# A graph network with LSTM windows on one core: block turns by VectorE and DMA, and seven-product LSTM steps summed in PSUM

## The chip, the cores and the metric

The kernel runs on one core of one Trainium2 chip, everything in 32-bit floats. The metric is the device time of one launch in microseconds; for the kernel before it is the median of three runs. A second number is the span of one profiled execution, from its first to its last instruction; the durations of single instructions all come from that execution.

## What is computed

The input `x` is 128 batches of 64 nodes with 256 features, with one 64 x 64 matrix `adj` for all. Four layers follow each other, each with a residual and a normalisation over the features:

```python
x = _layernorm(x + _L0_gnn_ref(x, adj, adj, W1, W2, W3))        # three products with adj*adj
x = _layernorm(x + _L1_gnn_ref(x, adj, W1, b1, W2, b2))         # eigenvectors U of a Laplacian
x = _layernorm(x + _L2_gnn_ref(x, adj, Wg0, ..., bih, bhh))     # two graph steps, then LSTMs
x = _layernorm(x + _L3_gnn_ref(x, adj, W, b_lin, b))            # attention over the 64 nodes
```

The LSTM part of the third layer is the largest. For p = 1, 2, 3, 4 in turn the 64 nodes of a batch are cut into windows of p rows; a one-layer LSTM with weights of its own runs over the p rows of each window, and its last hidden state replaces the window's last row:

```python
for p in range(1, MAX_SKIP + 1):
    wins = h[:, :nw * p, :].reshape(Bv * nw, p, Hd)
    last = _lstm_last(Wih[p - 1], Whh[p - 1], bih[p - 1], bhh[p - 1], wins)
    h = h.at[:, jnp.arange(nw) * p + (p - 1), :].set(last.reshape(Bv, nw, Hd))
```

One step is `g = x_t @ Wih.T + h @ Whh.T + bias`, split into the gates i, f, g, o, and then `c = sig(f)*c + sig(i)*tanh(g)`, `h = sig(o)*tanh(c)`. The first step of a window has no h and no old c, so it needs only i, g and o.

## The kernel before, in words

All 8192 rows (batch times node) are cut into 16 groups of 512 rows, four tiles of 128 rows each. The kernel has two stages. The first, to about 861 us, is layer 0 for all groups, with the eigenvectors worked out on VectorE beside it. The second takes the groups through layers 1, 2 and 3; the change is there alone.

In the second stage nothing is issued at once. `unit` records the work of two groups (the last four groups are units of one) as operations with a cost and the tiles they read and write; `Plan.run` then picks, engine by engine, the operation that can start earliest by its own account of times, with at most three units under way, and issues it. So the order of instructions on every engine is fixed when the program is built. Tiles live in a fixed number of slots per kind: 8 PSUM banks (`ps`), work tiles of 1024 columns (`w`, `WIDE` of them) and of 512 (`v`), `gates`, `c`, `hs`, and two attention tiles (`att`). `MOST` says how many of a kind are kept for the oldest unit. DMAs of this stage are issued from SP, in the planned order. All planned instructions carry line 156, so the profile's groups are told apart by tiles and shapes.

For a group, `layer1` multiplies with the eigenvectors (tiles `u2`, `ut2`). `to_lstm` makes `hT`, the features on the partitions and (node, batch) along a row. `lstm(hT, p, first, nw)` runs the windows of p rows step by step: for each gate and each half h of the 256 hidden features, two matmuls with `wih` and, from the second step on, two with `whh`, into a bank of its own; ScalarE reads the bank with the bias and applies tanh (the sigmoids are written through tanh), and VectorE does the rest. p = 1 is done in two calls of 256 columns, p = 2 in 256 columns, p = 3 in 168, and p = 4 in 128 columns per group.

For the second step of p = 2, and for steps two to four of p = 4 in units of two groups (`four`), `halves` takes the place of the direct matmuls. It cuts weights (two halves of inputs, two of outputs) and columns (two halves w) into a 2 x 2 block product and forms it from seven products instead of eight: sums of weight blocks are made once (`add_weights`), sums of the moving operands each step on VectorE, and the products go two to a bank, where ScalarE (`u1`) or VectorE picks them up and adds them into the `gates` tile.

Afterwards `from_lstm` brings `hT` back to rows: two copies on VectorE and two on ScalarE reorder it, eight TensorE transposes (a transpose is a TensorE instruction with `ident`, into a bank) turn it, and VectorE adds it to the rows. `layer3` needs three more turns: 8 transposes for `xT`, 8 for `hn` (the rows of h, with the bias `d_b` added) and 4 for the attention weights `e`, each with a copy or an add out of a bank. `norm` forms the statistics on VectorE and the root on GpSimd.

Of the kernel before, what the change touches and what calls it, by code (L numbers as in the profile page):

```python
# [99 lines left out]
class Op:  # L100
    __slots__ = ("engine", "calls", "cost", "lag", "before", "left", "after", "tiles", "start", "group", "rank", "ready", "unit")


class Plan:
# [7 lines left out]
    MOST = {"w": 4, "v": 2, "ps": 4, "gates": 2, "hs": 2}  # L112
# [11 lines left out]
    def note(self, engine, calls, cost, ready=0.0):  # L124
# [5 lines left out]
        for name, args, kw in () if callable(calls) else calls:  # L130
            for i, x in enumerate(list(args) + list(kw.values())):
                if not isinstance(x, Part):
                    continue
                t, write = x.tile, i == 0
                mask = np.zeros(int(np.prod(t.shape[1:])), bool)

                mask[... if t.tag == "ps" and not write else x.at.reshape(-1)] = True
                for other, w, rows, m in t.past:
                    if (w or write) and other is not op and other.start is None and rows[0] < x.rows[1] and x.rows[0] < rows[1] and (m & mask).any():
                        op.before.add(other)  # L140
                t.past.append((op, write, x.rows, mask))
                if t not in op.tiles:
                    op.tiles.append(t)
                    t.left += 1
        op.left = len(op.before)
# [12 lines left out]
    def run(self, units, ways):  # L158
# [4 lines left out]
        def rank(op):  # L163
            if op.engine == "PE" and not todo and len(left) <= LASTS:
                return -left[op.group]
            return op.group or 99

        def candidates(guard):
            oldest = min([u for u in going if u] or [0])
            best = None  # L170
            for e, ops in able.items():
                first = []
                for op in ops:
                    t = max(self.free[e], op.ready)
                    for tile in op.tiles:
                        if tile.real is None and tile.slot is None:
                            s = self.slots[tile.tag]
                            t = max(t, min(s))

                            if (guard and op.unit != oldest and  # L180
                                    sum(x < 1e9 for x in s) <= self.MOST.get(tile.tag, 1) - held.get((oldest, tile.tag), 0)):
                                t = 1e9
# [9 lines left out]
        while todo or going:  # L192
            while todo and len(going) < ways + (0 in going):
# [3 lines left out]
                going[self.unit] = len(self.ops)  # L197
                for op in self.ops:
# [544 lines left out]
GATES = 5  # L743
# [3 lines left out]
LASTS = 3  # L747
SINGLE = 4

# [58 lines left out]
def kernel(  # L808
# [92 lines left out]
    sqT2 = keep.tile([P, P], F32, name="sqT2")  # L901
    rs_row = keep.tile([P, P], F32, name="rs_row")
# [9 lines left out]
    dbl = load(keep, "dbl", d_bl, "p (k o) -> p k o", [P, 2, 1], o=1)  # L912
    cb1 = keep.tile([P, 2], F32, name="cb1")
# [209 lines left out]
    V.tensor_copy(rs_row, pr[:, :P])  # L1123
    V.tensor_reduce(rs_col, adst, AX.X, ALU.add)
    V.tensor_scalar(wide["c_b0"], wide["c_b0"], rs_col, None, op0=ALU.mult)
    V.tensor_add(cbi, cbi, cbh)
    for q in (slice(0, 4), slice(6, 8)):
# [23 lines left out]

    def place(tag, slot, shape):
        if tag == "att":
            return att[slot][:, :shape[1], :]
        if tag == "ps":
            return tl(psb, shape, f"ps{slot}")
        if tag in ("w", "v", "gates", "c", "hs"):
# [4 lines left out]
                {"ps": 8, "w": WIDE, "v": 4, "gates": GATES, "c": CELLS, "hs": OUTS, "att": ATT, "mx": 4, "sm": 4, "st": 4, "mv": 4,  # L1162
# [8 lines left out]
    def quarters(w):  # L1171
        w = w.rearrange("p k (a b h m) -> p k a b h m", a=2, b=2, h=2)
        return [w[:, k, :, b] for b in range(2) for k in range(2)]

    ways = {}

    def add_weights(p, ready):
        ways[p] = []
        for k, w in enumerate((wih[p - 1], whh[p - 1])):

            i = int(p == 2 and k == 1)
            s = wb.tile([P, 4 - i, 2, 2, P], F32, name=f"sums{p}{k}")
            s, w = plan.tile("sums", [P, 4 - i, 2, 2, P], s), plan.tile("sums", [P, 2, 1024], w)
            a11, a12, a21, a22 = quarters(w)
            S1, S2, S4, S3 = [s[:, j] for j in range(4 - i)] + [a21] * i
            V.tensor_add(S1, a21, a22, ready=ready)
            V.tensor_sub(S2, S1, a11, ready=ready)
            V.tensor_sub(S4, a12, S2, ready=ready)
            V.tensor_sub(S3, a11, a21, ready=ready)
            ways[p].append([a11, a12, a22, S1, S2, S3, S4])  # L1190

    def products(calls):
# [3 lines left out]
        plan.note("PE", [("matmul", (o, l, r), {"start": a, "stop": z}) for o, l, r, a, z in calls], cost)  # L1196
# [35 lines left out]
    def norm(x, scalar):  # L1232
# [4 lines left out]
        G.tensor_scalar(rs, mv[:, :, 1], EPS, None, op0=ALU.add)  # L1237
# [12 lines left out]
    def layer1(xs):  # L1250
# [14 lines left out]
        for t in range(0, 4, 2):  # L1265
# [4 lines left out]
            norm(xs[:, t:t + 2, :], False)  # L1270

    def to_lstm(xs):
        a = mixed(xs, adT2)
# [16 lines left out]
        for p, first, nw in ((1, 0, 32), (1, 32, 32), (2, 0, 32), (3, 0, 21)):  # L1290
            lstm(hT, p, first, nw)
        return hT

    def from_lstm(xs, hT, g):
        hb = as3(work(), 2)
        for bs in (slice(0, 4), slice(4, 8)):
            for k, copy, cost in ((0, V.tensor_copy, 0.33), (1, S.copy, 0.56)):
                copy(as3(hb[:, k, :], 8)[:, bs, :], hT[:, k, :, bs].rearrange("p n b -> p b n"), cost=cost)
        for t in range(0, 4, 2):
            p = ps4((P, 2, D))  # L1300
            turns([(p[:, j, k * P:(k + 1) * P], hb[:, k, (t + j) * P:(t + j + 1) * P]) for j in range(2)
                   for k in range(2)])
            V.scalar_tensor_tensor(xs[:, t:t + 2, :], p, 0.5, xs[:, t:t + 2, :], op0=ALU.mult, op1=ALU.add)
            norm(xs[:, t:t + 2, :], g in ENDING)

    def layer3(xs, g, first, nt):

        tiles = range(first, first + nt)

# [6 lines left out]
        xT = part(work(), 2)  # L1316
        ps = [ps4() for _ in range(2)]
        for t in tiles:
            turns([(ps[k][:, cols(t)], xs[:, t, k * P:(k + 1) * P]) for k in range(2)])
        if g in ENDING:  # L1320
            S.copy(xT[:, 0, :], ps[0][:, :nt * P])
        else:
            V.tensor_copy(xT[:, 0, :], ps[0][:, :nt * P])
        S.copy(xT[:, 1, :], ps[1][:, :nt * P])
        hT = part(work(), 2)
        for c in range(2):
            p = ps4()[:, :nt * P]
            run(p, [(dw[:, k, c * P:(c + 1) * P], xT[:, k, :]) for k in range(2)])
            S.activation(hT[:, c, :], p, AF.Identity, bias=dbl[:, c, :])
        p = ps4((P, nt, N))  # L1330
# [15 lines left out]
        V.tensor_sub(s, s, mx.unsqueeze(2).to_broadcast([P, nt, N]))  # L1346
        e = plan.tile("att", [P, nt, P])
        for h in range(2):
            hs = slice(h * N, (h + 1) * N)
            S.activation(e[hs, :, hs], s[hs, :, :], AF.Exp, cost=0.215 + 0.00042 * nt * N)  # L1350
        hn = part(work(), nt)
        for t in range(0, nt, 2):
            p = ps4((P, 2, D))
            turns([(p[:, j, c * P:(c + 1) * P], hT[:, c, (t + j) * P:(t + j + 1) * P]) for j in range(2)
                   for c in range(2)])

            V.tensor_add(hn[:, t:t + 2, :], p, wide["d_b"].unsqueeze(1).to_broadcast([P, 2, D]))
        sm = plan.tile("sm", [P, 4])[:, :nt]
        p = ps4()[:, :nt * P]
        turns([(p[:, t * P:(t + 1) * P], e[:, t, :]) for t in range(nt)])  # L1360
        eT = work2()[:, :nt * P]
        S.copy(eT, p)
        V.tensor_reduce(sm, e, AX.X, ALU.add)
        V.reciprocal(sm, sm)
        for t in range(0, nt, 2):
            p = ps4((P, 2, D))
            for j in range(2):
                run(p[:, j, :], [(eT[:, (t + j) * P:(t + j + 1) * P], hn[:, t + j, :])])
# [4 lines left out]
            norm(x2, g in ENDING)  # L1373
# [4 lines left out]
    def lstm(hT, p, first, nw, c=None, new=None):  # L1378
# [5 lines left out]
        only, hs = c is not None, None  # L1384
        for t in range(1 if only else p):
# [4 lines left out]
            if p == 2 and t:  # L1390
                x = [[xt[k][:, 16 * w:16 * w + 16] for w in range(2)] for k in range(2)]
                halves(2, x, hs.rearrange("p k (w n) -> p k w n", w=2), c.rearrange("p h (w n) -> p h w n", w=2), None,
                       lambda h, w: hT[:, h, 32 * w + 1:32 * w + 32:2, :])
                return
# [4 lines left out]
            if p > 1 and not t and not only:  # L1399
                c = plan.tile("c", [P, 512])[:, :2 * n].rearrange("p (h n) -> p h n", h=2)  # L1400
            if not only:
                new = None if last else plan.tile("hs", [P, 512])[:, :2 * n].rearrange("p (h n) -> p h n", h=2)
            for h in range(2):
                for q in names:
# [12 lines left out]
                    if q == "g":  # L1417
                        to = gate[h]["g"] if t or p == 1 else c[:, h, :]
# [7 lines left out]
                        S.activation(gate[h]["i"], c[:, h, :] if p > 1 else to, AF.Tanh, scale=0.5)  # L1426
# [12 lines left out]
    def halves(p, x, hs, c, new, rows):  # L1439
# [3 lines left out]
        bias = cbi[:, p - 1, :]  # L1443

        G = [plan.tile("gates", [P, 1024]).rearrange("p (w m q n) -> p w m q n", w=2, m=2, q=2) for _ in range(2)]
        both = work().rearrange("p (s i n) -> p s i n", s=2, i=4)

        def eights(v):
            return v.rearrange("p (w b) -> p w b", b=8)

        y = [[eights(hs[:, k, w]) for w in range(2)] for k in range(2)]
# [146 lines left out]
```

## Time and profile before

| | us |
|---|---|
| three runs: lowest, median, highest | 2457.69, 2458.52, 2458.81 |
| span of the profiled execution | 2455.8 |
| busy ScalarE, 860 to 1000 us | 72.19 of 140.00 |
| busy VectorE, 860 to 1000 us | 84.40 of 140.00 |
| busy TensorE, 2200 to 2400 us | 200.00 of 200.00 |
| one copy of 128x512 out of a bank: VectorE, ScalarE | 0.683, 0.583 |
| one add of 128x256 from a bank into `gates`, VectorE | 0.417 |
| one activation of 128x256 out of a bank, ScalarE | 0.473 |
| out rows, 128 KB, from issue to landing | 1.8 |
| `rest<-XA` and `X<-rest`, 512 KB, from issue to landing | 2.6, 3.3 |

Rows of the profile name an engine (PE is TensorE, PEld its weight loads, DVE VectorE, ACT ScalarE, POOL GpSimd, SP the queue that issues DMAs), the busy time in us and, after an x, the number of instructions. A matmul of 32-bit floats appears as two instructions, a transpose as one. TensorE's instructions overlap, so the duration of one is longer than the distance to the next.

### The profile page before, as it was taken

The page shows a single profiled execution, that of the slowest core. Times are in us where ns is not written, and L with a number is a line of the kernel's source. Part 1 is how long each engine was busy: PE and PEld are TensorE (multiplying, and loading weights), DVE is VectorE, ACT ScalarE, POOL GpSimd, SP SyncE. Part 2 cuts the span into 40 slices and gives each one's busy share as a digit, 9 for nine tenths or more (in the row PEclk, how much of TensorE's full clock was granted, in tenths as well). Part 3 has the DMA queues.
Part 4 walks back from the last instruction along what each step waited for, and adds up shares of the span by engine and source line. Part 5 has one row for each costly group of instructions (what it writes and reads, how often), then busy time and mean ns, then how long its engine had stood idle before and what let it go on. Part 6 is the DMA issues. An engine that isn't in the chain of part 4 may idle for free.

```text
span 2455.8 us, 40814 instructions
## 1 busy us (share of the span) xinstructions
PE 2431.6 (99%) x15500; PEld 2158.3 (88%) x15500; DVE 1618.6 (66%) x5676; ACT 1073.0 (44%) x2610; POOL 137.5 (6%) x315
## 2 busy tenths in 40 slices
PE   9999999999999999999999999999999999999997
PEld 7888888878887899989989998998998998988996
DVE  6888877778888265584684486477558458374336
ACT  2333433333333354445444445444444444545555
POOL 0000000000000010010010000001001001010002
PEclk9999999999999999999999999999999999999999
DMA  7000000000000020010000001001001000000000
GB/s 227 9 1 18 9 10 10 9 10 9 9 1 1 35 87 1 1 36 1 1 18 18 1 1 35 1 1 36 1 1 35 1 1 18 1 10 1 1 1 27
DMA packets 27972, 42.69 MB, mean 17 GB/s; under 512 B 2944, under 2 KB 22144, under 8 KB 27776
## 3 DMA queue, kind: packets, MB, share of 16 engines
q1 hardware_dynamic: 27424, 39.81, 4.7%
q8 instruction: 122, 2.00, 0.3%
q14 instruction: 74, 0.61, 0.1%
q10 hardware_dynamic: 352, 0.28, 0.0%
HBM read 26.45 MB, written 13.63 MB: 16 GB/s over the span
## 4 chain that ended last, share of the span: by engine, by line
PE 94%; DVE 4%; DMA 1%; ACT 0%; issue 0%; POOL 0%; SPq 0%; ACTq 0%; POOLq 0%; DVEq 0%
PE ps L156 62%; PE ps L940 31%; DVE D L52 1%; DVE X L156 1%; PE pc L296 1%; DMA XA<-in_x_dram 1%; DVE st L156 0%; DVE tw L52 0%; POOL rs L156 0%; DVE w L156 0%; DVE h L52 0%; ACT gates L156 0%; DVE gates L156 0%; DVE u L52 0%; DVE v L156 0%
## 5 line engine op out<-in xcount | busy, mean ns | idle before, releaser
L156 PE MATMUL ps<-w,wih 128*128 128x128 f32 (+2 forms) x4144 | 752.7, 315 | 0.9 <-DVE gates L156 0.9
L156 PEld LDWEIGHTS ps<-w,wih 128*128 128x128 f32 x4144 | 646.5, 191 | 37.0 <-issue 6.7
L156 ACT ACTIVATE gates<-ps,cbi 128x168 f32<-128x168 f32 (+2 forms) x832 | 342.2, 417 | 361.2 <-PE ps L156 353.0
L156 PE MATMUL ps<-hs,whh 128*128 128x168 f32 (+1 forms) x1952 | 345.1, 291 | 0.0
L156 PEld LDWEIGHTS ps<-hs,whh 128*128 128x128 f32 x1952 | 288.9, 191 | 1.2 <-issue 1.0
L156 PE MATMUL ps<-w,sums 128*128 128x128 f32 x1776 | 237.7, 275 | 0.0
L940 PE MATMUL ps<-aw,h 128*128 128x256 f32 x1024 | 227.2, 379 | 0.0
L156 DVE SCALAR_TENSOR_TENSOR gates<-gates 128x256 f32<-128x256 f32 (+2 forms) x220 | 83.9, 382 | 215.7 <-ACT gates L156 215.1
L156 PEld LDWEIGHTS ps<-w,sums 128*128 128x128 f32 x1776 | 218.1, 192 | 1.5 <-issue 1.2
L940 PEld LDWEIGHTS ps<-aw,h 128*128 128x128 f32 x1024 | 192.9, 190 | 25.9 <-ACT h L949 0.5
L156 ACT ACTIVATE gates<-gates,cbi 128x256 f32<-128x256 f32 x272 | 116.2, 497 | 194.6 <-DVE gates L156 194.6
L949 ACT ACTIVATE h<-h 128x512 f32<-128x512 f32 x128 | 80.4, 629 | 196.3 <-DVE h L52 196.1
L156 DVE TENSOR_TENSOR gates<-gates,ps 128x256 f32<-128x256 f32 x340 | 128.4, 417 | 19.4 <-PE ps L156 14.4
L940 PE MATMUL ps<-ss,tw 128*128 128x256 f32 x512 | 117.9, 380 | 0.0
L940 PE MATMUL ps<-ss,aw 128*128 128x256 f32 x512 | 117.3, 379 | 0.0
L940 PE MATMUL ps<-m,aw 128*128 128x256 f32 x512 | 117.1, 380 | 0.0
L156 DVE SCALAR_TENSOR_TENSOR c<-gates,c 128x256 f32<-128x256 f32 (+2 forms) x156 | 57.1, 366 | 87.2 <-ACT gates L156 87.0
L940 PE MATMUL ps<-aw,m 128*128 128x512 f32 x256 | 114.6, 593 | 0.0
L156 DVE TENSOR_TENSOR gates<-v,ps 128x256 f32<-128x256 f32 x136 | 55.6, 417 | 80.7 <-ACT v L156 49.9
L940 PEld LDWEIGHTS ps<-ss,aw 128*128 128x128 f32 x512 | 96.6, 190 | 12.8
L940 PEld LDWEIGHTS ps<-ss,tw 128*128 128x128 f32 x512 | 96.3, 190 | 12.9 <-issue 0.2
L940 PEld LDWEIGHTS ps<-m,aw 128*128 128x128 f32 x512 | 95.6, 190 | 12.6 <-issue 0.5
(314 smaller groups left out, 3734.7 us busy)
## 6 DMA issues: line engine op xcount, KB each, us to landing
out_dram<-X SPq DMA_DIRECT2D x64, 128.0 KB, 1.8
rest<-XA SPq DMA_DIRECT2D x10, 512.0 KB, 2.6
X<-rest SPq DMA_DIRECT2D x10, 512.0 KB, 3.3
XA<-in_x_dram SPq DMA_DIRECT2D x18, 256.0 KB, 6.0
wih<-in_c_ih_dram SPq DMA_DIRECT2D x4, 1024.0 KB, 7.4
aw<-in_a_w_dram SPq DMA_DIRECT2D x3, 1024.0 KB, 10.8
X<-in_x_dram SPq DMA_DIRECT2D x12, 256.0 KB, 5.9
whh<-in_c_hh_dram SPq DMA_DIRECT2D x3, 1024.0 KB, 9.4
```

The lines of the kernel that those rows point to most:

```text
L52: return getattr(self.engine, name)(out, *args, **kw)
L156: getattr(e, name)(*[real(x) for x in args], **{k: real(v) for k, v in kw.items()})
L296: PE.matmul(out, lhsT, rhs, start=True, stop=True)
L940: PE.matmul(out, lhsT, rhs, start=start, stop=stop)
L949: S.activation(dst, src, AF.Relu)
```

## The change

Two things change, both in the second stage.

First, in the 14 groups that are not in `ENDING`, TensorE's transposes are replaced. VectorE's transpose turns each 32 x 32 block of a tile by itself; the blocks are then put in order by DMA: `across` writes the tile to a buffer in device memory (`far`, eight of them) and reads it back in four pieces into another work tile. `from_lstm` does so once, `layer3` twice, and for the attention weights eight small DMAs place the turned blocks straight into the `att` tile. The softmax is now formed on the unturned tile.

Second, the seven-product form is used for all steps but p = 3 (and p = 4 in the four units of one group): for p = 1, for both steps of p = 2 and all four of p = 4. `fast` replaces `halves`. It sums inside the banks: product 1 goes into `chain`, ScalarE copies it out for a first block, product 6 is added on top in the same bank, it is copied out again, then 7, an add, then 4. A second bank takes product 2, a third 5 and then, on top, 3. Products go in gate by gate, all gates of a pass side by side in one bank. The four planned numbers for slots and the rank by which the planner picks (`due`, a time before which an operation should start, counted in `PERIOD` per group) change with it. Smaller edits: a factor of one half moves into `adH2` and the normalisation, `dbb` adds two biases, and a list of plain ordering edges is given to the leftover normalisations of the first stage.

```diff
-    MOST = {"w": 4, "v": 2, "ps": 4, "gates": 2, "hs": 2}
+    MOST = {"w": 3, "v": 2, "ps": 2, "gates": 3, "hs": 2}
...
-            return op.group or 99
+            return op.due
...
+                for op in reversed(self.ops):
+                    op.tail = op.cost + max([x.tail + (self.OWN if x.engine == op.engine else self.LAG)[op.engine]
+                                             for x in op.after] or [0.0])
+                    op.due = op.group * PERIOD - op.tail
...
-GATES = 5
+NARROW = 3
+GATES = 6
+PERIOD = 25.0
+FARS = 8
...
+    def across(src):
+        far = plan.tile("far", [P, 1024])
+        Q.dma_start(far, src, cost=0.6)
+        dst = work()
+        for j in range(4):
+            Q.dma_start(dst[32 * j:32 * j + 32].rearrange("r (i f) -> r i f", i=4),
+                        seen(far[:, 256 * j:256 * j + 256], "(i r) f -> r i f", i=4), cost=0.6)
+        return dst
...
+        z = work()
+        for k in range(2):
+            V.transpose(z.rearrange("p (j t k f) -> p t j k f", j=4, t=4, k=2)[:, :, :, k],
+                        hT[:, k].rearrange("p n b -> p b n"))
+        y = across(z).rearrange("p (i m f) -> p m i f", i=4, m=8)
...
-        for p, first, nw in ((1, 0, 32), (1, 32, 32), (2, 0, 32), (3, 0, 21)):
-            lstm(hT, p, first, nw)
+        singles(hT)
+        pairs(hT)
+        lstm(hT, 3, 0, 21)
...
+            S.activation(s, s, AF.Exp)
+            V.tensor_reduce(sm, s, AX.X, ALU.add)
+            z = sc.rearrange("p a c -> p (a c)")[:, 256:]
+            V.transpose(z.rearrange("p (b t r) -> p t b r", b=2, t=4), s)
+            for h in range(2):
+                for b in range(2):
+                    for a in range(2):
+                        Q.dma_start(e[64 * h + 32 * b:64 * h + 32 * b + 32, :, 64 * h + 32 * a:64 * h + 32 * a + 32],
+                                    z[64 * h + 32 * a:64 * h + 32 * a + 32, 128 * b:128 * b + 128]
+                                    .rearrange("p (t r) -> p t r", t=4), cost=0.6)
...
-            p1, p2 = two(0, 1)
-            S.copy(u1, p1)
-            V.tensor_add(a, u1, p2)
-            p6, p7 = two(5, 6)
-            V.tensor_add(c12, u1, p6)
-            V.tensor_add(b, c12, p7)
-            p5, p3 = two(4, 2)
-            V.tensor_add(d, b, p5)
-            V.tensor_add(c12, c12, p5)
-            V.tensor_add(c12, c12, p3)
-            p4, _ = two(3)
-            V.tensor_add(b, b, p4)
+            chain, bank2, bank5 = ps4(shape), ps4(shape), ps4(shape)
+            c11, c12, c22 = block[0][:, :, 0], block[0][:, :, 1], block[1][:, :, 1]
+            product(chain, 1, qs, True, (block[0], bank2))
+            S.copy(c11, chain)
+            product(bank2, 2, qs, True)
+            V.tensor_add(c11, c11, bank2)
+            product(chain, 6, qs, False)
+            S.copy(c12, chain)
+            product(bank5, 5, qs, True)
+            S.copy(c22, bank5)
+            product(chain, 7, qs, False)
+            V.tensor_add(c22, c22, chain)
+            product(bank5, 3, qs, False)
+            V.tensor_add(c12, c12, bank5)
+            product(chain, 4, qs, False)
...
+        fast(1, 256, [[hT[:, k, 32 * w:32 * w + 32, :] for w in range(2)] for k in range(2)], write=write)
...
+        fast(2, 128, x[0], c=c, new=hs)
+        fast(2, 128, x[1], hs=hs, c=c, write=write)
...
-        for w in range(2):
-            lstm(hTs[w], 4, 0, 16, c[:, :, w, :], hs[:, :, w, :])
-        for t in range(1, 4):
+        for t in range(4):
             x = [[hTs[w][:, k, t:t + 61:4, :] for w in range(2)] for k in range(2)]
             new = state("hs") if t < 3 else None
-            halves(4, x, hs, c, new, lambda h, w: hTs[w][:, h, 3:64:4, :])
+            fast(4, 128, x, hs, c, new, write)
             hs = new
```

## The prediction, made before the run

> **What bounds the kernel now.** I read the page's span and busy shares first, then the busy time by stretches, then the waits of TensorE alone, then the groups kept apart by shape, last the timeline of TensorE for the true distance between matmuls.
>
> ```profile
> span 2455.8 us, 40814 instructions
> PE 2431.6 (99%) x15500; PEld 2158.3 (88%) x15500; DVE 1618.6 (66%) x5676; ACT 1073.0 (44%) x2610; POOL 137.5 (6%) x315
> PE 94%; DVE 4%; DMA 1%; ACT 0%; issue 0%; POOL 0%; SPq 0%; ACTq 0%; POOLq 0%; DVEq 0%
> ...
> 1000.00:2200.00 1200.00, 1197.85 (x8703) 1104.53 (x8702) 761.44 (x2240) 555.41 (x1320) 77.88 (x156) 1.00 0.03 11
> 2400.00:2456.00 56.00, 40.12 (x329) 33.08 (x327) 39.98 (x137) 28.96 (x71) 15.00 (x40) 0.91 0.09 29
> ...
> PE ps L156 <- DVE w L156: 1.0, 3, 0.4
> PE ps L156 <- DVE gates L156: 0.9, 1, 0.9
> ```
>
> TensorE is busy 2431.6 of 2455.8 us at full clock, and 94% of the chain that ended last is TensorE. The stretch from 1000 to 2200 us has 1197.85 of 1200 us busy, with VectorE at 63% and ScalarE at 46%. The last two lines are all of TensorE's waits between 860 and 2400 us: 1.9 us. So there the time is the sum of the matmuls. The one loose place is the last 56 us, where TensorE idles 15.9 us: the last groups alone, one dependency after another.
>
> A busy row alone could hide pipelining, so I take the cost of a matmul from the distance between starts:
>
> ```profile
> 958.96 9.66 PE L156 MATMUL ps<-w,wih 128*128 128x256 f32 x44
> 968.46 1.46 PE L156 MATMUL ps<-bw,v 128*128 128x256 f32 x6
> ...
> 1017.02 2.84 PE L156 MATMUL ps<-w,wih 128*128 128x128 f32 x24
> 1019.70 1.50 PE L156 MATMUL ps<-adT,w 128*128 128x128 f32 x12
> ...
> 2404.76 1.91 PE L156 MATMUL ps<-ident,w 128*128 128x128 f32 x16
> 2406.51 0.61 PE L156 MATMUL ps<-w,wih 128*128 128x128 f32 x4
> ```
>
> 256 columns: (968.46 - 958.96)/44 = 0.216 us; 128 columns: 2.68/24 = 0.1117 us; a transpose: 1.75/16 = 0.109 us. A matmul of the program is two of these instructions (1152 records of the 256-column form for 576 in the built program), so 0.4315 us and 0.2234 us; a transpose is one. Priced so, everything TensorE has after the first `u2` matmul at 860.96 us comes to 1585 us; it took until 2442.57 us, 1581.6 us. The prices hold to 0.2%.
>
> [...]
>
> **The change, part by part, on TensorE.** Counts are from the two built programs.
> - p = 1 (`singles`): 24 matmuls of 256 columns per group become 7 products x 3 gates = 21: 16 groups x 3 x 0.4315 = -20.7 us.
> - p = 2, first step: 12 of 256 become 21 of 128, 16 x (12 x 0.4315 - 21 x 0.2234) = -7.8 us.
> - p = 4, first step of six units: 24 of 128 become 21, -18 x 0.2234 = -4.0 us.
> - The later steps of p = 2 and p = 4 had seven products already: 0. p = 3 and the p = 4 steps of the four single groups stay as they are: 0.
> - Transposes: per group 8 in `from_lstm`, 8 + 8 + 4 in `layer3`; 28 x 14 groups x 0.109 = -42.7 us.
>
> Sum: **-75.2 us** of TensorE work.
>
> **On the other engines**, which must only stay below TensorE. VectorE: 428 gate sums of 256 columns out of a bank go (0.417 us: -178); 150 of 512 (0.68) and 66 of 384 (0.55, between its neighbours) come (+139). The block turns are 56 of 512 and 70 of 256 columns; taken like a 512-column pass (0.68) and a 256-column one (0.41), +67 us; bounds: [...] twice my price, +134. The copies and adds after TensorE's transposes go (-42); operand sums for the new seven-product steps come (+52); the pointwise gate operations become fewer and wider (-18). Net some +20 us on 1619. ScalarE: 264 copies out of banks come (0.365 to 0.585 us, +136) for 68 that go (-25), gate activations in other sizes (+18), fewer copies after transposes (-20); net some +110 us on 1073, which takes it from 46% to about 56% in the steady stretch, VectorE from 63% to about 67%. Neither bounds.
>
> **Waits that come.** First, the bank re-entries: 88 passes (32 for p = 1, 32 for p = 2, 24 for p = 4) x 4 = 352 places where a product goes into a bank that ScalarE or VectorE has just read. Behind the waiting matmul stands all of TensorE's order. The reader starts about 0.21 us after the last matmul (in before, matmuls ending at 1001.29 by distance, the activation at 1001.50) and takes 0.585 (copy of 512) or 0.68 us (add), so 0.8 to 0.9 us must be filled. In the built order I summed the matmuls between each bank's last write before a read and its next write: the median is 1.2 us above the need, and only 3 of 352 fall short, by 1.2 us in all. That assumes a reader that is free at once. Low end 0; high end a mean 0.3 us each, 106 us; I take 3 us, since readers at 56% and 67% will sometimes be a little late and 17 places have under 0.1 us to spare.
>
> Second, the turns: 42 of them, each a write of 512 KB (2.6 us by the row of `rest<-XA`) and four reads of 128 KB (the row `X<-rest`, 512 KB, took 3.3), and 14 times eight small copies into the attention tile, at 0.37 to 0.47 us each to issue on SP by the four weight loads at 860 us: about 3.4 us plus 1.9 to land. All are issued in order on SP, where a turn that waits for its write holds up the next group's turns, the output rows and the reload of X, and behind those stand the group's own products. A group's way lengthens by some 3 x 6 us minus what the transposes and copies took. While it waits, TensorE has two other units of two groups each; before, it idled 2 us in 1540 with the same number. The turns move 42 x 1.05 = 44 MB, 28 GB/s over the 1530 us in question, beside 227 GB/s in the first slice: bandwidth is no issue. Low end 0, high end one half turn per group uncovered, 14 x 2.5 = 35 us; I take 3.
>
> Third, the end: groups 14 and 15 keep TensorE's transposes, so the same chain closes the kernel, but in the built order all 56 of their transposes now stand after the last LSTM matmul, with 27 us of TensorE work there. I take 4 us more idle there (between 0 and 8). At the start, the sums of the weights of p = 1 are 8 short VectorE operations, under 5 us, while TensorE has layer 1 of several groups: 0.
>
> **Sum.** 2455.8 - 75.2 + 3 + 3 + 4 = 2390.6 us for the span. The median lies 2.7 us above the profiled span, so **2393 us**.
>
> **Rivals.**
> 1. Nothing is given back: 2458.5 - 75.2 = 2383 us. For it: the fill computed above. Against: the planned order assumes transfers and readers on time. 0.13.
> 2. The turns take the place of the transposes: one half turn per group uncovered, 2383 + 35 + 10 = 2428 us. For it: SP's single order, seven large work tiles that are now held while DMAs land. Against: the present 2 us of waits. 0.16.
> 3. Slower: the bank reads. TensorE stops at each of the 352 re-entries until ScalarE or VectorE has read; from a mean stop of 75/352 = 0.21 us on the gain is gone, and at 0.3 us the time is 2383 + 106 = 2489 us. For it: ScalarE's longer queue, and an order that cannot move aside. Against: the fill, and single stops must be large to make that mean. 0.10.
>
> My forecast has 0.61, its own range 2384 to 2412.
>
> **How the numbers follow.** The range runs from 2378 (rival 1 with a little less at the end) to 2432 (rival 2), leaving out rival 3 and a few per cent. Under 0.2%, 5 us, no change can be told: 0.02, from rival 2's far end. Faster: 0.61 + 0.13 + 0.14 = 0.88; slower 0.10.
>
> **What will show it.** TensorE busy near 2357 us (right price of the removed work). Its waits for ScalarE and VectorE gates, 0.9 us now, below 15 (rival 3 if over 75). Its waits for DMA-written work tiles near 0 (rival 2 if over 25). Idle of TensorE in the last 56 us near 20. VectorE's turn of 512 columns near 0.68 us. I am wrong if TensorE shows idle spread through the middle slices.

## The result, and the profile after

The changed kernel takes 2466.37 us (median of 5 runs, 2463.69 to 2470.08) beside 2458.81 us for the kernel before (5 runs, 2457.69 to 2459.22): a ratio of 1.0033, 95% interval 1.002 to 1.0045. It is 0.3% slower, where 2393 us was forecast; the time lies outside the range. The profiled execution took 2464.81 us, its span 2463.0.

The page of the changed kernel, its parts on the span, the busy shares, TensorE's slices and the chain that ended last:

```profile
span 2463.0 us, 41136 instructions
...
PE 2386.0 (97%) x15264; PEld 2112.1 (86%) x15264; DVE 1639.9 (67%) x5562; ACT 1143.9 (46%) x2838; POOL 137.5 (6%) x315
...
PE   9999999999999999999999999998998998999996
...
PE 83%; DVE 10%; DMA 3%; ACT 2%; issue 1%; SPq 1%; POOL 0%; DVEq 0%; ACTq 0%; POOLq 0%
```

TensorE's share of the chain fell from 94% to 83%; VectorE went from 4% to 10%, DMA from 1% to 3%, and SP's queue from 0% to 1%. The slices with an 8 begin in the second half. Busy time by stretches of the changed kernel (after the length of the stretch: TensorE, weight loads, VectorE, ScalarE and GpSimd, then the granted TensorE clock, the DMA share and GB/s):

```profile
1000.00:2200.00 1200.00, 1152.71 (x8419) 1060.58 (x8418) 757.00 (x2084) 613.68 (x1523) 75.08 (x148) 0.99 0.15 45
2200.00:2400.00 200.00, 196.35 (x1473) 186.86 (x1472) 100.17 (x278) 104.39 (x274) 5.96 (x12) 0.99 0.06 20
2407.00:2463.00 56.00, 36.95 (x290) 30.47 (x288) 32.64 (x117) 26.21 (x66) 12.16 (x36) 0.83 0.16 50
```

Between 1000 and 2200 us TensorE is idle 47.3 us where it was idle 2.2, and it issues 284 instructions fewer there. In the last 56 us it is idle 19.1 us. So the time is lost in the middle, not at the end. TensorE's waits between 860 and 2400 us in the changed kernel (us in total, times, longest), of nine rows that sum to 50.8 us:

```profile
PE ps L160 <- DVE gates L160: 17.6, 13, 3.3
PE ps L160 <- DVE w L160: 13.6, 10, 3.3
PE ps L160 <- DMA w<-far: 9.5, 5, 3.6
...
PE ps L160 <- DMA att<-v: 2.0, 1, 2.0
```

And from VectorE's waits in the changed kernel, the row for the tiles that come back from device memory:

```profile
DVE X L160 <- DMA w<-far: 15.7, 10, 4.8
```

The rows name mostly VectorE as what TensorE waits for, and only 11.5 us are put down to a DMA. The timeline shows what such a wait can be. One turn of `hT` in the changed kernel (start, duration, engine, operation; in brackets the idle time before it and what ended it):

```profile
2161.73 2.09 DVE L160 STREAM_TRANSPOSE w<-w 128x512 f32<-128x512 f32 x2
...
2163.85 0.33 SPq L160 DMA_DIRECT2D far<-w  x1
...
2167.19 1.75 SPq L160 DMA_DIRECT2D w<-far  x4
...
2169.47 0.39 PE L160 MATMUL ps<-hs,sums 128*128 128x128 f32 x2
2171.80 0.69 DVE L160 TENSOR_TENSOR X<-w,X 128x512 f32<-128x512 f32 x1 [4.78 <-DMA w<-far]
2172.41 0.68 DVE L160 TENSOR_TENSOR gates<-gates,ps 128x512 f32<-128x512 f32 x1
...
2173.14 0.49 PE L160 MATMUL ps<-w,wih 128*128 128x128 f32 x2 [3.28 <-DVE gates L160]
...
2173.47 0.39 PE L160 MATMUL ps<-w,whh 128*128 128x128 f32 x2
...
2173.69 0.39 PE L160 MATMUL ps<-w,wih 128*128 128x128 f32 x2
...
2174.80 0.64 PE L160 MATMUL ps<-w,wih 128*128 128x128 f32 x2
...
2175.23 0.63 PE L160 MATMUL ps<-w,whh 128*128 128x128 f32 x2
```

The write is issued at 2163.85, the reads follow 3.3 us later, when it has landed, and VectorE can add the turned tile at 2171.80: 8.0 us after the write's issue, 10.1 us after the turn began. In VectorE's order this add, for which VectorE was idle 4.78 us, stands ahead of the gate sum that empties the bank for TensorE's next product. TensorE's last matmul before the stop starts at 2169.47, but the sum runs only at 2172.41, behind the add. The profile calls this a wait for `gates`; the transfer held it up. It is a turn that stops a bank re-entry.

The last four lines show a second cost. Two instructions take 0.22 us from start to start at first (2173.47 to 2173.69), and 0.43 from 2174.80: after the stop, TensorE ran at half its clock (granted 0.50 from 2174.4 to 2177.6). Over the whole span the mean granted clock is 0.989; before, it was 0.998. Stretches of the changed kernel around this stop, columns as above:

```profile
2165.00:2173.00 8.00, 4.86 (x44) 4.67 (x42) 1.89 (x3) 0.12 (x1) 0.00 (x0) 1.00 0.38 116
2173.00:2181.00 8.00, 7.30 (x48) 7.11 (x49) 7.00 (x22) 5.39 (x16) 0.89 (x2) 0.79 0.00 1
2181.00:2190.00 9.00, 9.00 (x63) 8.79 (x63) 8.15 (x25) 4.22 (x12) 1.79 (x6) 1.00 0.16 61
```

The new operations, from the changed kernel's groups kept apart by shape (after the form: busy us, mean ns of one, idle time before and what ended it) and, below, its DMA issues (KB each, median us from issue to landing):

```profile
L160 DVE STREAM_TRANSPOSE w<-w 128x512 f32<-128x512 f32 x28 | 30.2, 1096 | 0.0
...
L160 DVE STREAM_TRANSPOSE w<-X 128x256 f32<-128x256 f32 x56 | 20.4, 413 | 0.0
...
L160 DVE STREAM_TRANSPOSE w<-v 128x512 f32<-128x512 f32 x28 | 19.8, 707 | 25.9 <-ACT v L160 22.0 <-issue 3.8
...
L160 DVE STREAM_TRANSPOSE v<-v 128x256 f32<-128x256 f32 x14 | 6.1, 439 | 3.5 <-ACT v L160 3.5
```

```profile
far<-w SPq DMA_DIRECT2D x42, 512.0 KB, 2.6
w<-far SPq DMA_DIRECT2D x168, 128.0 KB, 3.0
...
att<-v SPq DMA_DIRECT2D x112, 16.0 KB, 1.8
```

The turn of `hT` reads its source with a step of eight floats and takes 1.096 us; of the same 512 columns read side by side it takes 0.707.

### The profile page after: what moved, and what is told of

The parts are those of the page before. It is cut to its first block, busy times and chain, and to the rows that moved or that the text cites. A ratio compares the mean times of both kernels' runs of the same rounds, so it can differ in the third digit from the quotient of the medians.

```text
span 2463.0 us, 41136 instructions
## 1 busy us (share of the span) xinstructions
PE 2386.0 (97%) x15264; PEld 2112.1 (86%) x15264; DVE 1639.9 (67%) x5562; ACT 1143.9 (46%) x2838; POOL 137.5 (6%) x315
## 4 chain that ended last, share of the span: by engine, by line
PE 83%; DVE 10%; DMA 3%; ACT 2%; issue 1%; SPq 1%; POOL 0%; DVEq 0%; ACTq 0%; POOLq 0%
PE ps L160 50%; PE ps L956 31%; DVE w L160 2%; ACT gates L160 2%; DVE gates L160 2%; DMA w<-far 2%; DVE X L160 1%; SPq L160 1%; DVE c L160 1%; DVE st L160 1%; DVE D L52 1%; PE pc L307 1%; DVE v L160 1%; DMA XA<-in_x_dram 1%; DMA far<-w 0%
## 5 line engine op out<-in xcount | busy, mean ns | idle before, releaser
L160 PE MATMUL ps<-w,wih 128*128 128x128 f32 (+2 forms) x3708 | 659.1, 301 | 30.7 <-DVE gates L160 17.6
L160 PEld LDWEIGHTS ps<-w,wih 128*128 128x128 f32 x3708 | 552.4, 193 | 67.0 <-DVE gates L160 24.3
L160 ACT ACTIVATE gates<-ps,cbi 128x128 f32<-128x128 f32 (+2 forms) x722 | 261.0, 387 | 234.2 <-PE ps L160 228.4
L160 PE MATMUL ps<-w,sums 128*128 128x128 f32 (+1 forms) x2368 | 345.9, 289 | 1.7 <-ACT gates L160 1.2
L160 PEld LDWEIGHTS ps<-w,sums 128*128 128x128 f32 x2368 | 305.2, 192 | 13.4 <-issue 2.9
L160 ACT ACTIVATE gates<-gates,cbi 128x256 f32<-128x256 f32 (+2 forms) x500 | 207.5, 477 | 154.2 <-DVE gates L160 154.0
L160 DVE TENSOR_TENSOR gates<-gates,ps 128x512 f32<-128x512 f32 (+2 forms) x264 | 156.5, 601 | 174.4 <-PE ps L160 165.5
L160 ACT COPY gates<-ps 128x512 f32<-128x512 f32 (+2 forms) x264 | 135.4, 521 | 182.3 <-PE ps L160 179.1
L160 DVE SCALAR_TENSOR_TENSOR c<-gates,c 128x256 f32<-128x256 f32 (+2 forms) x156 | 56.7, 364 | 124.5 <-ACT gates L160 124.0
L160 DVE SCALAR_TENSOR_TENSOR gates<-gates 128x256 f32<-128x256 f32 (+3 forms) x188 | 78.9, 420 | 86.9 <-ACT gates L160 85.8
L160 POOL TENSOR_SCALAR rs<-mv 128x2 f32<-128x2 f32 x96 | 24.4, 264 | 1474.5 <-DVE mv L160 1457.0
```

Of the source, the lines that this page charges most:

```text
L160: getattr(e, name)(*[real(x) for x in args], **{k: real(v) for k, v in kw.items()})
```

## The experiments

Two theories stood at first. A: the turns cost the time, partly because the planner prices them too low and so writes an order that the chip cannot keep. B: the re-entries of the banks cost it. To compare runs, I add up from each trace how much longer the distance between TensorE instructions was than the distances worked out in the prediction, after 860 us ("stops"; the time at half clock is in it). All times are medians, the ratios are to the kernel before beside them.

| run | this, us | runs | ratio, 95% interval | stops, us |
|---|---|---|---|---|
| before (profile) | | | | -1.8 |
| after | 2466.37 | 5 | 1.0033 (1.002 to 1.0045) | 86.5 |
| e1_cost | 2458.29 | 12 | 1.0002 (0.9993 to 1.001) | 76.3 |
| e2_products | 2440.14 | 4 | 0.993 (0.9914 to 0.9947) | 12.2 |
| e3_turns | 2534.71 | 4 | 1.0315 (1.03 to 1.033) | 123.1 |
| e4_lag | 2442.11 | 4 | 0.9936 (0.9921 to 0.9951) | 61.1 |
| e5_prices | 2442.40 | 4 | 0.9938 (0.9922 to 0.9955) | 60.2 |
| e6_products_prices | 2436.74 | 4 | 0.9916 (0.9902 to 0.9931) | 9.7 |
| e7_layer3 | 2514.76 | 4 | 1.0236 (1.022 to 1.0251) | 124.0 |
| e8_hback | 2473.47 | 4 | 1.0064 (1.0049 to 1.0079) | 59.6 |
| e9_no_trip | 2420.46 | 4 | 0.9847 (0.9833 to 0.9862) | 41.0 |
| e10_no_blocks | 2417.83 | 4 | 0.9837 (0.9822 to 0.9852) | 35.0 |
| e11_most | 2520.42 | 4 | 1.0255 (1.0238 to 1.0272) | 142.6 |
| e12_x_turn | 2436.17 | 4 | 0.9912 (0.9897 to 0.9927) | 20.2 |
| e13_neither | 2389.64 | 4 | 0.9725 (0.971 to 0.9739) | 8.5 |
| e14_att_pe | 2436.37 | 4 | 0.9921 (0.9904 to 0.9937) | 52.0 |

In each of them the planner writes a new order, so a difference holds what an edit does to the order as well as what it does itself. How much the order alone can do is shown by e4 and e11, which have the instructions of the changed kernel: 2442.11 and 2520.42 us.

### One half of the change at a time

e2_products keeps the seven-product steps and gives every group TensorE's transposes again:

```diff
     def from_lstm(xs, hT, g):
-        if g in ENDING:
+        if True:
...
-        ending = g in ENDING
+        ending = True
...
```

> The seven-product steps alone: all 16 groups keep TensorE's transposes and their copies, in the form that the last two groups have in the changed kernel. TensorE's priced work in the second stage is 1552 us against 1509 in the changed kernel and 1585 before. Theory A: no waits for DMA-written tiles are left, TensorE's stops fall under 15 us, time 2425 to 2440 us. Theory B (bank re-entries stop TensorE): stops of 50 us or more remain, time 2475 us or more.

It takes 2440.14 us, with 12 us of stops. The stretch by busy time of this run:

```profile
1000.00:2200.00 1200.00, 1192.53 (x8910) 1106.43 (x8909) 732.55 (x2041) 650.09 (x1589) 74.06 (x148) 1.00 0.03 11
```

The same 352 re-entries are in it, and TensorE idles 7.5 us in 1200. All its stops together are 12.2 us, so this bounds what the re-entries can cost in this order. Theory B falls.

e3_turns keeps the turns and has the LSTM steps of before, with the rank and the slot numbers that belong to them (the main lines of its difference from the changed kernel):

```diff
-    MOST = {"w": 3, "v": 2, "ps": 2, "gates": 3, "hs": 2}
+    MOST = {"w": 4, "v": 2, "ps": 4, "gates": 2, "hs": 2}
...
-            return op.due
+            return op.group or 99
...
-NARROW = 3
-GATES = 6
+NARROW = 4
+GATES = 5
...
-        singles(hT)
-        pairs(hT)
-        lstm(hT, 3, 0, 21)
+        for p, first, nw in ((1, 0, 32), (1, 32, 32), (2, 0, 32), (3, 0, 21)):
+            lstm(hT, p, first, nw)
...
```

> The block turns alone: LSTM steps, planner numbers and rank of the kernel before, turns by VectorE and DMA in 14 groups. TensorE's priced work in the second stage is 1541 us. Theory A: the turns cost about as much in stops as they take from TensorE, 2440 to 2475 us. Theory B: nearly all of the 43 us is kept, about 2420 us.

It takes 2534.71 us, 77.5 us above its kernel before, though 43 us of transposes are gone. TensorE's waits between 860 and 2330 us in this run:

```profile
PE ps L160 <- DMA w<-far: 36.1, 6, 15.9
PE ps L160 <- DVE w L160: 18.6, 4, 7.7
PE ps L160 <- DMA att<-v: 9.0, 5, 5.4
```

Here the products themselves wait for the transfers, once for 15.9 us. So the turns lose time without the new LSTM steps too, and in this older order more than I expected of either theory.

### The planner's prices

The planner takes 0.60 us for the strided turn, where the distance to the next instruction was 1.02. For a DMA it takes 0.6 us to issue and 2.0 more to land (`LAG`), so it counts on a turned tile 7.0 us after the write's issue (2.6 for the write, 4 x 0.6 + 2.0 for the reads), where the trip above took 8.0. Comparing the other planned costs with the trace, one is systematically short: an activation with a bias out of a work tile, by 0.074 us (256 columns: 0.399 us to the next start, planned 0.325), 272 of them before and 500 after. e1_cost mends the turn alone, e4_lag the DMA alone, e5_prices all three, e6_products_prices the activation in e2:

```diff
-                        hT[:, k].rearrange("p n b -> p b n"))
+                        hT[:, k].rearrange("p n b -> p b n"), cost=1.03)
```

```diff
-    LAG = {"PE": 0.205, "DVE": 0.13, "ACT": 0.14, "POOL": 0.0, "SP": 2.0}
+    LAG = {"PE": 0.205, "DVE": 0.13, "ACT": 0.14, "POOL": 0.0, "SP": 4.0}
```

```diff
+                if name == "activation" and not bank and "bias" in kw:
+                    cost += 0.074
...
-    LAG = {"PE": 0.205, "DVE": 0.13, "ACT": 0.14, "POOL": 0.0, "SP": 2.0}
+    LAG = {"PE": 0.205, "DVE": 0.13, "ACT": 0.14, "POOL": 0.0, "SP": 3.0}
...
+                        hT[:, k].rearrange("p n b -> p b n"), cost=1.03)
```

> The same instructions as the changed kernel, in another planned order: the planner is told 1.03 us instead of 0.60 us for the two 512-column block turns of hT in from_lstm, whose measured mean is 1.096 us. Theory A (VectorE's order goes wrong at from_lstm: the turns of hT run about 1 us longer per group than planned, the adds of the turned tile then wait for the DMA at the head of VectorE's queue, and the gate sums behind them reach TensorE late): VectorE's wait for w<-far falls from 15.7 us to under 8, TensorE's waits for gates and w from 31 us to under 15, time 2415 to 2440 us. Theory B (the re-entries of the banks): VectorE's prices elsewhere are unchanged, time within 10 us of 2466.

> The changed kernel with one planner number altered: a DMA is planned to be usable 4.0 us after its issue instead of 2.0, which covers the 1 us of the long turns and the 3.0 us that the reads take to land. Same instructions, another order. Theory A: the adds of the turned tile are placed later on VectorE, its wait for w<-far falls under 5 us, time 2410 to 2440 us. Theory B: no gain, or a loss of some us since work tiles are planned to be held longer, 2460 to 2480 us.

> The changed kernel, its planner given three measured prices: 1.03 us for the long turns, 0.074 us more for an activation with a bias out of SBUF, and 3.0 us instead of 2.0 from a DMA's issue to its use. Same instructions. Theory A (the order is wrong where the planner's prices are): better than either price alone, 2405 to 2430 us, TensorE's stops in the second stage under 45 us. Theory C (the turns lengthen each group's way so much that TensorE runs out of ready work, whatever the prices): no better than the 2442 us of the longer DMA time alone.

> Seven-product steps with TensorE's transposes (2440 us), the planner given the 0.074 us more for an activation with a bias out of SBUF. Theory A: a few us, 2432 to 2438. If ScalarE's late readers are no limit: 2438 to 2443.

e1 wins 8 us, e4 and e5 24 us; all three miss the times of theory A, e4 by 2 us. (e1 lies where theory B had put it, but e2 rules B out.) VectorE's wait for the turned tile, 15.7 us in the changed kernel, is in e1, e4 and e5

```profile
DVE X L160 <- DMA w<-far: 21.4, 10, 5.6
...
DVE X L160 <- DMA w<-far: 2.8, 2, 2.5
...
DVE X L160 <- DMA w<-far: 9.6, 8, 3.0
```

In e1 it rose, where theory A had it fall below 8, and e4 and e5 take the same time with 2.8 and 9.6 us of it. So 24 us of the loss go with the prices by which the order was planned, but this one wait does not measure them, and in e4 61 us of stops remain. For the rest I formed theory C: the turns lengthen each group's way until TensorE has too little ready, whatever the prices; e5 fits it. e6 gains 3 us on e2.

### One turn at a time

e8_hback has only the turn of `hT` by VectorE and DMA (`ending = True` in `layer3`); e7_layer3 the reverse (`if True:` in `from_lstm`), for which the planner found an order only with `MOST` for work tiles at 4; e11_most is the changed kernel with that number alone; e12_x_turn has the prices of e5 and only layer 3's first turn; e14_att_pe is e5 with only the attention weights back on TensorE.

```diff
-    MOST = {"w": 3, "v": 2, "ps": 2, "gates": 3, "hs": 2}
+    MOST = {"w": 4, "v": 2, "ps": 2, "gates": 3, "hs": 2}
```

```diff
+TURN_H, TURN_X, TURN_N, TURN_A = False, True, False, False
...
-        if g in ENDING:
+        if g in ENDING or not TURN_H:
...
+        px, pn, pa = last or not TURN_X, last or not TURN_N, last or not TURN_A
...
```

> The changed kernel with the turn of hT in from_lstm given back to TensorE (8 transposes, two copies on each of VectorE and ScalarE), the turns in layer3 kept, and one planner number (work tiles kept for the oldest unit: 4 instead of 3) since the planner finds no order otherwise. Priced TensorE work 1521 us, 12.5 more than in the changed kernel. Theory A (the turn of hT is the one that hurts, since gate sums of the LSTM stand behind it on VectorE): 2415 to 2440 us, stops under 40 us. Otherwise, if the turns of layer3 hurt as much: 2455 us or more.

> The other half: only the turn of hT in from_lstm by VectorE and DMA, layer3 by TensorE as in the last two groups. Priced work 1540 us. Theory A: the stops of the turn of hT remain, 40 us or more, 2455 to 2475 us. Otherwise: stops as in the kernel without turns (11 us), 2428 us.

> The changed kernel with MOST for work tiles 4 in place of 3, nothing else: the second edit that e7 had to carry. If e7 was slow because of it, this is slower than 2490 us; if the turns of layer 3 alone made e7 slow, this stays within 15 us of 2466.

> The seven-product steps with corrected prices (as e6, DMA lag 3.0), and of the turns only the first of layer 3 (xT): by VectorE and DMA; the other three stay on TensorE. It takes 112 transposes off TensorE, 12.2 us. If a turn costs as in e8 (33 us for one of the three): 2450 to 2460. If this one has slack, since its tile is read by products that are not urgent: 2428 to 2437, below e6.

> e5 with the attention weights turned on TensorE again (56 transposes, 6.1 us of TensorE work back; 14 VectorE turns of 256 columns and 112 small copies on SP go). If SP's issue of eight copies a group, 5 to 6 us in front of the next turn, carries a part of the 60 us: 2430 us or less. If not: 2442 to 2452.

The turn of `hT` alone takes 12.2 us of work from TensorE and makes e2 33 us slower (2473.47 against 2440.14): stops rise from 12 to 60 us. Both have the planner's old prices, so a part of the 33 us can be theirs. e7 read alone would say that layer 3's turns are worse still; e11 shows that it says nothing of them, since `MOST` at 4 by itself makes the changed kernel 54 us slower. With the prices right, layer 3's first turn breaks even: 12.2 us of work for 10 us more stops, 2436.17 beside 2436.74 us in e6 (the ranges, 2435.26 to 2436.92 and 2436.67 to 2437.78, overlap). e14 gives 6.1 us of transposes back to TensorE and is 6 us faster than e5, but 52 us of stops stay, and its time lies between the two that were expected: the small copies, with the 14 block turns that go with them, carry a part, the smaller one. Layer 3's second turn, of the rows of h, was not run alone.

### Trip and block turns taken apart

What is it about a turn: the trip through device memory, or VectorE's own work in the middle of a queue on which TensorE's next products hang? e9_no_trip leaves out the first, e10_no_blocks the second, e13_neither both; the prices are those of e5 and TensorE's work is that of the changed kernel.

```diff
     def across(src):
-        far = plan.tile("far", [P, 1024])
-        Q.dma_start(far, src, cost=0.6)
...
+        return src
```

```diff
-        z = work()
-        for k in range(2):
-            V.transpose(z.rearrange("p (j t k f) -> p t j k f", j=4, t=4, k=2)[:, :, :, k],
-                        hT[:, k].rearrange("p n b -> p b n"), cost=1.03)
-        y = across(z).rearrange("p (i m f) -> p m i f", i=4, m=8)
+        y = across(hT.rearrange("p k n b -> p (k n b)")).rearrange("p (i m f) -> p m i f", i=4, m=8)
...
-            xT = across(z).rearrange("p (j k t r) -> p k t j r", j=4, k=2, t=4)
+            xT = across(xs.rearrange("p t f -> p (t f)")).rearrange("p (j k t r) -> p k t j r", j=4, k=2, t=4)
...
-                h = work2()
-                S.activation(h, p, AF.Identity, bias=dbb[:, c, :])
-                V.transpose(z.rearrange("p (j t c f) -> p t j c f", j=4, t=4, c=2)[:, :, :, c], h)
+                S.activation(z[:, 512 * c:512 * c + 512], p, AF.Identity, bias=dbb[:, c, :])
```

> The changed kernel with the corrected prices (as e5), but the round trip of the block turns through device memory is left out: the block-turned tile is used as it is, so blocks are not put in order and the output is another. VectorE's turns, TensorE's work and the eight small attention copies stay. Theory C (the way through device memory, 7 us per turn, starves TensorE): 2385 to 2410 us, TensorE's stops beyond the pitch fall from 60 to under 30 us. Theory D (VectorE's own turning work, put in the middle of a queue on which TensorE's next products hang, starves it): 2430 to 2450 us, stops still 45 or more.

> The counterpart of e9: prices as in e5, the 42 round trips stay, but VectorE's turns of h and of the two tiles of layer 3 are left out (126 instructions in the full kernel, 76 us; the tile goes to device memory unturned, so the output is another). The turns of the attention weights stay. Theory C: no better than 2430 us, stops 45 or more. Theory D: 2390 to 2415 us, stops under 30 us. If both e9 and e10 fall, the two lie in one chain and neither alone is the cause; if neither falls, it is the small copies or the order.

> e9 and e10 together: prices as in e5, both the round trips and VectorE's turns of h and of the two tiles of layer 3 left out (the output is another); TensorE's work is that of the changed kernel, and the turns of the attention weights with their small copies stay. If trip and block turns each add their own stops, e9's 22 us and e10's 25 us add up: 2390 to 2400 us, which is where the prediction stood, and the fill of the bank reads is shown to hold in the full set of changes. If either one alone already makes the turn harmless: 2412 to 2418 us, and 20 us or more of stops come from the small copies or the order.

Beside e5 (2442.40 us), e9 wins 21.9 us, e10 24.6, and both together 52.8, a little more than their sum of 46.5. What e10 leaves out is 112 turn instructions of 70.4 us; the 126 and 76 us of its expectation count the 14 of the attention weights, which stay. So neither C nor its rival D holds alone: leaving out either takes stops away, leaving out both takes nearly all, and e9's and e10's stops of 41 and 35 us missed the bounds of 30 that I had set for either. The two shares are less firm than their sum: both are smaller than what another order alone can do (54 us in e11), and without a trip or without block turns the planner also needs fewer work tiles, which no run kept apart. The page of e13, and its stretch by busy time:

```profile
span 2386.8 us, 40579 instructions
...
PE 2359.9 (99%) x15264; PEld 2101.6 (88%) x15264; DVE 1575.7 (66%) x5450; ACT 1140.5 (48%) x2838; POOL 132.1 (6%) x315
...
PE   9999999999999999999999999999999999999997
```

```profile
1000.00:2200.00 1200.00, 1194.35 (x8861) 1109.30 (x8860) 737.59 (x2088) 644.40 (x1596) 74.17 (x156) 1.00 0.04 13
```

With the same 15264 TensorE instructions as the changed kernel, the same bank re-entries and the small attention copies, TensorE idles 5.7 us in these 1200 instead of 47.3, its clock is 1.00 there again (0.997 over the span), and the time is 2389.64 us, just under the 2390 to 2400 expected of it and 3 us from the prediction, which had 3 us for the turns in it. The way from the changed kernel to it is 76.7 us, 24.0 by the prices and 52.8 by trip and turns.

Of the kernels that compute the whole, e12 (2436.17), e14 (2436.37) and e6 (2436.74) are the fastest, and not told apart: some 0.8% below before. e6 is the simplest: the seven-product steps without any turn.

## Why the prediction was wrong

The sum was right but for one term, that of the turns.

- **TensorE's work, -75.2 us: right.** e13 has it all and ends 67.4 us below its kernel before. Its sign, TensorE busy near 2357 us, came in e13 (2359.9) and not in the changed kernel (2386.0), where up to 22 us are half clock (last section). The part for the products alone is 32.5 us (20.7 + 7.8 + 4.0); e6, which does just that, has 9.7 us of stops in place of -1.8 and ends 20.6 us below: 32.5 - 11.5 = 21.
- **Bank re-entries, 3 us: right in kind.** e2 has 12.2 us and e13 8.5 us of stops of every sort. In 352 places the changed kernel and e2 add a product to a bank after a read of its partial sum, where before has none, and both compute the whole; with the fill computed from the built order this cost 14 us at most in e2 (12.2 beside -1.8 before).
- **The turns, 3 us with a high end of 35: the step that failed.** The three large turns of each group cost 77 us (the changed kernel beside e13), 5.5 us for each of 14 groups; 24 us of them go with the planner's prices. The step saw the mechanism, SP's single order (in the changed kernel SP waited 69.5 us for its own writes to `far` between 860 and 2400 us, 34 times) and a way longer by some 18 us a group, an estimate, and then covered it with two other units because they had covered the shorter way before. That these had left 2 us of waits in 1540 said that the cover was enough for that way, not that there was any to spare. The high end of half a turn per group was a guess without a row behind it. One of its parts was also too small: the eight copies of a group hold SP for 5.1 to 7.8 us in the changed kernel, where the step had 3.4.
- **Where a turn waits.** I looked for waits of TensorE for DMA-written tiles, "near 0", and for gates, "below 15". They were 11.5 and 19.0 us, and would not have passed for rival 2 (over 25) or rival 3 (over 75), though rival 2's mechanism was at work. In the stop shown above, the wait lands on VectorE, whose add stands ahead of a gate sum, and the sum's lateness then shows under `gates`. How many of the stops come about in this way is not shown. The last sign, idle spread through the middle slices, is the one that came. I had asked what queues behind a waiting matmul and behind a waiting DMA on SP, not what queues behind the add on VectorE.
- **VectorE, "neither bounds": true as a share, wrong as a price of nothing.** Its turns took 76.5 us, not 67, for the strided ones cost 1.096 and not 0.68; it stays at 67% of the span. Still e10 shows that leaving out 70.4 us of them wins 25 us.
- **The planner's prices: not looked at.** Rival 1 was marked down because "the planned order assumes transfers and readers on time", but I did not work out what they are, though the rows at hand (3.3 us for `X<-rest`, where the code has 2.6 in all) said that they were short. Right prices are worth 24 us.
- **The end, 4 us: right.** 19.1 us idle in the last 56 us, where I said near 20.
- **The rivals.** 1 fell. 3 had the kernel slower, but its cause falls with e2. 2 had the cause with less than half its size: 35 us for the turns where 77 came.

What the runs don't settle is how the 53 us divide between a slower VectorE queue, a longer way and the tiles held meanwhile: each run has another planned order, and one with the changed kernel's order held still was not tried.

## What to carry to other kernels

Taking a step off the busiest engine and putting it on two engines that are not busy was not free here (77 us for the three large turns): it needs a cover for its latency that is shown to have room, and low waits before the change (1.9 us) showed that the present latency was covered, no more. A wait for a transfer can be paid by whatever stands behind it in an engine's order, as VectorE's 4.78 us came out as 3.28 us of TensorE, so name the instruction behind the consumer and who waits for that one. Where an order is planned from prices, measure the new operations first and put the right prices in: that was worth 24 us here, with one number (e4) as with three (e5).

## What was not expected of the hardware

A stop was dearer here than its length. In the second stage of the changed kernel TensorE's granted clock, as its trace records it, goes to half ten times, for 3.41 or 6.83 us, the last time from 2451 us to the end. Each of the eight that come before the last groups begins within 5 us of the start of a stop of 2.0 to 3.6 us, though not every such stop is followed by one (those of 2.0 us at 1285, 2.8 us at 1875 and 2.7 us at 2033 are not). In before this happened once, among the last groups, from 2446 us to the end. The span had 0.989 of the full clock where before had 0.998, which is up to 22 us (0.009 x 2463) and part of the stops above. What decides whether a stop is followed by the half clock is not shown.

VectorE's block turn of 32-bit floats took 0.707 us for 512 columns read side by side, and 1.096 with a step of eight floats; the code writes both in the same pattern. The prediction had priced 512 columns at 0.68 us: the first lies 0.03 us above that, the second 0.42 us.
